# A transformer block with linear attention and eight experts: modulation of the token rows moved behind the dispatch, LayerNorm statistics moved to ScalarE, a running sum moved to GpSimd

## The chip, the cores and the metric

The kernel runs on one core of one Trainium2 chip. The metric is device time in microseconds (us). Before the change the median of six runs is 1135.47 us (1133.32 to 1144.9). Engines are named as in the profile: PE is TensorE (matmul and transpose), PEld its weight loads, DVE is VectorE, ACT is ScalarE, Pool is GpSimd, and SP is SyncE, which here only issues DMAs.

## The reference

There are 8192 tokens (4 batches of 2048) of D = 256 features, all in fp32. Six modulation rows per batch come from the condition c. Then:

```python
mod = (silu(c) @ wmod).reshape(4, 6, 1, 256)
sa, ca, ga, sb, cb, gb = mod[:, 0], ..., mod[:, 5]
ga, gb = sign(ga) * max(|ga|, 0.25), sign(gb) * max(|gb|, 0.25)
h = layernorm(x) * (1 + ca) + sa
q, k, v = phi(h @ wq.T), phi(h @ wk.T), h @ wv.T      # phi = elu + 1, 16 heads of 16
# along each sequence: S += k v^T, z += k, out = (S q) / max(z . q, 1e-6)
x = x + ga * (out @ w_out.T)
h = layernorm(x) * (1 + cb) + sb
gates = softmax(h @ w_router.T)                        # 8 experts, the best 2 of each token,
# 1280 places per expert, given out in token order; the kept gates are made to sum to 1: combine
hidden = silu(h @ w_gate.T)                            # 512 features, shared by the experts
x = x + gb * sum_e combine[:, e] * (hidden @ w_down[e].T)
```

## The kernel before, in words

**Setup.** It loads weights, computes the modulation, and keeps it in three forms: `modc` (columns, for data that has features on partitions), `gab` (rows of ga and gb) and `scb` (rows of sb and 1 + cb).

**Token stage.** The tokens are taken in 16 groups `g` of 512, each of four tiles `j` of 128; four groups make a batch. A loop over steps `s` = (g, j) runs under an order written out by hand for PE, ACT, DVE and Pool: an engine executes its instructions in just the order in which the loop writes them. Step (g, j) does the attention of tile j: `scores` (psc, masked by DVE at L419), `attend` of the step before (po, copied to oT by ACT at L472), `keep_state` (a matmul `pst`, added to the running sum `s_acc` by DVE at L442, then masked to `s_msk` by Pool at L444), and `project_out` (pw at L485, the add into x, and the statistics of the second LayerNorm). Between these stand pieces of other groups, by j:

| step | next group g+1 | g+2 and g+3 | group before, g-1 | g-2 |
|---|---|---|---|---|
| j=0 | q, first running keys | g+2: normalise a (L287) on ACT | spread of the second norm | |
| j=1 | `kk` copies (L354), values | g+3: load of x on SP | normalise m on ACT | `positions` (L574), `dispatch` |
| j=2 | denominators `den` (L382), scaled q (`pr`) | g+2: `hTa` (L300); g+3: statistics on DVE | `hTm`; row inputs of two tiles on Pool | sends of two tiles |
| j=3 | | g+2: k | logits, `ranks` on DVE; row inputs of two tiles | sends of two tiles |

Here a is the first LayerNorm, m the second. Its statistics are bn_stats and bn_aggr on DVE, then `ve` (DVE), the power `rstd` (Pool) and `nmr` (DVE, L278); normalise is one ACT instruction per tile with scale and bias, and the transposes of `to_features` follow on PE, whose copy to SBUF (`hTa`, `hTm`) applies the modulation as columns. Most matmul results of this stage share one PSUM ring, `bank`, of two buffers, so a result that is read late holds up the matmul after the next.

**Rows.** For the experts, `row_inputs` (L491) writes each token's row into `hrow` on Pool: normalised x times 1 + cb plus sb (two operations a tile, L502 and L503), gb, the combine weights and the token number; W = 2D + 12 = 524 floats. `send` (L626) scatters the rows, 128 per indirect DMA on Pool's queue, into `slots` in DRAM, 1280 for each expert. Blank rows are put there first: `free_slots` (L618) issues 80 blocks of 128 rows on SP, eight at each of the steps 2 to 11, each behind the mask of that step. The sends wait for all of them.

**Experts' stage.** Its order is the scheduler's. Each expert has three blocks of 4, 4 and 2 tiles: `rows` are loaded on SP (L646; a ring `e3` of five buffers), DVE casts the token numbers `tok` (L657), Pool gathers the tokens' present output `xc` (L660), PE transposes the rows (`pte`, L676, copied by ACT at L677), then `ph` (L682), tanh on ACT (L690), `hid` on DVE (L691), `pe` (L696), on DVE `y` (L703, times combine weight and gb) and the add of `xc` (L707), and a scatter to the output on Pool (L708).

## Time and profile before

The profiled execution took 1141.07 us, with a span of 1139.3 us and a mean granted clock of 0.919. It counts 17805 instructions. Busy times by stage, from the windows of the trace, in us (share of that stage for PE):

| stretch (us) | PE | DVE | ACT | Pool | clock | DMA share |
|---|---|---|---|---|---|---|
| 0 to 100, setup and start | 72.4 (72%) | 46.2 | 28.3 | 21.7 | 0.91 | 0.16 |
| 100 to 400, tokens | 252.6 (84%) | 198.6 | 123.7 | 148.2 | 0.93 | 0.37 |
| 400 to 700, tokens | 248.0 (83%) | 204.2 | 120.9 | 165.0 | 0.92 | 0.16 |
| 700 to 770, last tokens | 50.3 (72%) | 44.9 | 16.7 | 42.3 | 0.84 | 0.12 |
| 770 to 814, drain | 5.8 (13%) | 11.2 | 3.8 | 22.8 | 0.50 | 0.17 |
| 814 to 1139, experts | 305.2 (94%) | 131.4 | 73.9 | 159.1 | 0.98 | 0.42 |
| whole span | 934.3 (82%) | 636.5 (56%) | 367.3 (32%) | 558.8 (49%) | 0.919 | |

How to read it: an engine is limited by its own work only where its busy time fills the stretch. The clock is that of PE, as a share of full speed. The DMA issues of the page: 80 blank blocks of 262 KB (3.7 us to landing), 16 loads of rows of 1048 KB (7.3 us), 16 loads of x of 512 KB (3.9 us), 128 sends. In all 110.69 MB go through the queues.

### The profile page before, as it was taken

To read this page: it belongs to the slowest core of one execution; us is meant where nothing else is said; L and a number is where in the kernel's file an instruction comes from. 1 tells how busy PE (TensorE), PEld (TensorE's weight loads), DVE (VectorE), ACT (ScalarE), POOL (GpSimd) and SP (SyncE) were. 2 spreads that over 40 slices of the span, in tenths; PEclk is the share of its full clock that TensorE was granted. 3 is DMA by queue.
4 is the path that set the end of the run, shared out by engine and by line. 5 is a ranking of instruction groups with operands and counts; after the bars stand their busy time and mean duration, and the time that the engine had idled before them with its cause. 6 is when DMAs were issued, how large, how long until landed. Compare 5 with 4: busy or idle time off the path is not lost. (4 is left out here: it accounts for less than half of the span.)

```text
span 1139.3 us, 17805 instructions
## 1 busy us (share of the span) xinstructions
PE 934.3 (82%) x6832; PEld 662.2 (58%) x6832; DVE 636.5 (56%) x1448; ACT 367.3 (32%) x738; POOL 558.8 (49%) x690
## 2 busy tenths in 40 slices
PE   5878988788887887887987879762499999999996
PEld 5546666556656555565665566541275666666664
DVE  3446565775676676756767757662243444434443
ACT  0344533344334343444344343111122222221221
POOL 4012343484473663644745636665534555535553
PEclk9889998999898998989989889785699999999998
DMA  5004775221122121211111000011524443544321
GB/s 185 1 1 143 268 247 213 76 95 62 56 92 76 57 95 47 86 50 66 69 45 58 31 32 31 31 33 50 200 85 156 159 158 113 163 164 140 126 76 51
DMA packets 62902, 110.69 MB, mean 97 GB/s; under 512 B 9934, under 2 KB 30670, under 8 KB 62816
## 3 DMA queue, kind: packets, MB, share of 16 engines
q1 hardware_dynamic: 39040, 59.71, 15.7%
q0 software_dynamic: 17920, 42.48, 10.7%
q10 hardware_dynamic: 5856, 7.35, 2.0%
q8 instruction: 54, 0.88, 0.3%
q14 instruction: 32, 0.26, 0.1%
HBM read 47.69 MB, written 74.68 MB: 107 GB/s over the span
## 5 line engine op out<-in xcount | busy, mean ns | idle before, releaser
L696 PE MATMUL pe<-wd,hid 128*128 128x256 f32 x640 | 158.7, 385 | 10.2 <-DVE hid L691 8.3
L626 POOL DMA_INDIRECT slots<-hrow,idx x128 | 131.6, 1028 | 54.3 <-issue 42.5
L419 DVE TENSOR_TENSOR at<-psc,tri 128x1024 f32<-128x1024 f32 x128 | 150.2, 1214 | 13.1 <-PE psc L413 13.0
L682 PE MATMUL ph<-hTe,wg_sb 128*128 128x512 f32 (+1 forms) x384 | 153.3, 527 | 0.0
L485 PE MATMUL pw<-wob,oT 128*128 128x256 f32 x256 | 83.5, 456 | 80.9 <-ACT kk L354 41.9
L444 POOL TENSOR_TENSOR s_msk<-s_acc,bd 128x256 f32<-128x256 f32 x60 | 49.5, 826 | 202.0 <-DVE s_acc L442 197.5
L696 PEld LDWEIGHTS pe<-wd,hid 128*128 128x128 f32 x640 | 116.1, 189 | 54.8 <-DVE y L703 16.1
L708 POOL DMA_INDIRECT out_dram<-y,tok x80 | 78.5, 981 | 95.4 <-DVE y L707 54.2
L485 PEld LDWEIGHTS pw<-wob,oT 128*128 128x128 f32 x256 | 51.3, 215 | 109.2 <-ACT kk L354 35.1
L660 POOL DMA_INDIRECT xc<-out_dram,tok x80 | 80.6, 1007 | 69.7 <-issue 45.4
L690 ACT ACTIVATE th<-ph 128x512 f32<-128x512 f32 (+1 forms) x96 | 50.4, 526 | 189.6 <-PE ph L682 138.7
L682 PEld LDWEIGHTS ph<-hTe,wg_sb 128*128 128x128 f32 x384 | 70.9, 191 | 44.0 <-issue 30.8
L691 DVE SCALAR_TENSOR_TENSOR hid<-th,ph 128x512 f32<-128x512 f32 (+1 forms) x96 | 56.9, 595 | 57.3 <-ACT th L690 49.7
L703 DVE SCALAR_TENSOR_TENSOR y<-pe,rows 128x256 f32<-128x256 f32 x80 | 38.6, 483 | 85.8 <-PE pe L696 61.5
L413 PE MATMUL psc<-qeo,k 32*128 32x256 f32 x1024 | 74.3, 404 | 9.5 <-DVE at L419 9.5
L329 PE MATMUL pv<-wqkv_sb,hTa 128*128 128x256 f32 x256 | 73.6, 451 | 0.9 <-DVE x L486 0.9
L369 POOL TENSOR_TENSOR zq<-zc,q 128x512 f32<-128x512 f32 x32 | 41.4, 1295 | 65.5 <-DVE zc L364 57.2
L464 PE MATMUL po<-at,vpad 128*32 128x128 f32 x2048 | 71.3, 279 | 0.2
L314 PE MATMUL pk<-hTa,wqkv_sb 128*128 128x512 f32 x128 | 65.6, 639 | 5.0 <-ACT rek L320 4.5
L329 PEld LDWEIGHTS pv<-wqkv_sb,hTa 128*128 128x128 f32 x256 | 59.9, 235 | 13.7 <-DVE x L486 1.7
L464 PEld LDWEIGHTS po<-at,vpad 128*32 128x32 f32 x2048 | 53.3, 111 | 22.4 <-issue 21.9
L314 PE MATMUL pq<-hTa,wqkv_sb 128*128 128x512 f32 x128 | 61.4, 605 | 3.7 <-ACT req L320 3.6
(148 smaller groups left out, 1540.4 us busy)
## 6 DMA issues: line engine op xcount, KB each, us to landing
slots<-free SPq DMA_DIRECT2D x80, 262.0 KB, 3.7
rows<-slots SPq DMA_DIRECT2D x16, 1048.0 KB, 7.3
x<-in_x_dram SPq DMA_DIRECT2D x16, 512.0 KB, 3.9
out_dram<-x SPq DMA_DIRECT2D x16, 512.0 KB, 4.5
rows<-slots SPq DMA_DIRECT2D x8, 524.0 KB
wd<-in_wdT_dram ACTq DMA_DIRECT2D x8, 512.0 KB, 4.0
slots<-hrow,idx POOLq DMA_INDIRECT x128
wmod_sb<-in_wmod_dram ACTq DMA_DIRECT2D x1, 1536.0 KB
```

Source lines behind the costliest of these rows:

```text
L314: nc.tensor.matmul(pq, wqkv_sb[:, k, o + h * P : o + (h + 1) * P], hT[:, k, :], start=(k == 0), stop=(k == NH - 1))
L329: nc.tensor.matmul(pv[:, i * D : (i + 1) * D], hT[:, k, (j + i) * P : (j + i + 1) * P], wqkv_sb[:, k, 2 * D : 3 * D], start=(k == 0), stop ...
L413: nc.tensor.matmul(psc[:, a, h], kT[r : r + 32, h, cols], qeo[r : r + 32, h, :, cols], start=True, stop=True,)
L419: masked = nc.vector.tensor_tensor(at, psc[:, 2 * m : 2 * m + 2].rearrange("p i h q t -> p (i h q) t"), tri.unsqueeze(1).to_broadcast([P, ...
L464: nc.tensor.matmul(po[32 * a : 32 * a + 32, h * P : (h + 1) * P], vp[:, j, h * 4 + a, q : q + 2, :], att[a // 2][:, a % 2, h, q, :], start ...
L485: nc.tensor.matmul(pw[:, :D], oT[:, h, :], wob[:, h, :], start=(h == 0), stop=(h == NH - 1))
L626: row = nc.gpsimd.indirect_dma_start(out=slots[:, :], out_offset=bass.IndirectOffsetOnAxis(ap=idx[:, c, j : j + 1], axis=0), in_=hr[:, j, ...
L660: got = nc.gpsimd.indirect_dma_start(out=xc[:, i + j, :], out_offset=None, in_=out[:, :], in_offset=bass.IndirectOffsetOnAxis(ap=tok[:, j ...
L682: nc.tensor.matmul(ph[:, :m], wg_sb[:, k, f * P : (f + 1) * P], hT[:, k, :m], start=(k == 0), stop=(k == NH - 1),)
L691: nc.vector.scalar_tensor_tensor(hid[:, f, :m], th[:, :m], 1.0, ph[:, :m], ALU.add, ALU.mult)
L696: nc.tensor.matmul(pe[:, j, :], hid[:, f, j * P : (j + 1) * P], wds[e][:, f, :], start=(f == 0), stop=(f == NF - 1),)
L708: put = nc.gpsimd.indirect_dma_start(out=out[:, :], out_offset=bass.IndirectOffsetOnAxis(ap=tok[:, j : j + 1], axis=0), in_=y[:, j, :], in ...
```

## The change

1. **Rows.** A row now carries normalised x without modulation, and beside it the batch's rows 1 + cb, sb and gb: W = 4D + 12 = 1036 floats, 4144 bytes for 2096. `gab` and `scb` become one tile `modr`. `row_inputs` is gone; ACT's normalise m writes straight into the row, Pool copies the three modulation rows into it only for the first two groups of a batch (there are two `hrow` buffers). The experts' stage multiplies and adds on DVE ahead of the transposes, two instructions per block, into a new tile `hm`. The ring of row buffers goes from five to four.
2. **Statistics.** Those of the first LayerNorm leave DVE: ACT adds up x (`sums`, an Identity with an accumulated output, for g+3 at j=3), Pool makes the negative mean, ACT adds up the squared differences (`squares`, for g+2 at j=0, where normalise a stood), and Pool makes `ve`, the power and `nmr`. Normalise a moves to j=1, behind the values. The small operations of the second LayerNorm move from DVE to Pool.
3. **State.** ACT copies `pst` to SBUF (`s_add`), and Pool adds it to `s_acc`.
4. **Blank blocks.** `free_slots` moves forward: two batches of eight behind group 0's first k, two behind group 1's, then one at each odd step from 1 to 11.
5. **Room.** relu writes into its destination (no `re` tile), `zq` shares the tile of `qs`, and `ahead` and `tie` have one buffer.

```diff
-O_GB, O_CW, O_TOK, W = D, 2 * D, 2 * D + NE, 2 * D + NE + 4
+O_CB, O_SB, O_GB, O_CW, O_TOK, W = D, 2 * D, 3 * D, 4 * D, 4 * D + NE, 4 * D + NE + 4
...
+    def sums(g):
+        xn = G_["xna", g] = w1.tile([P, NT, D], F32, tag="xna", name=f"xna_{g}")
+        sm = small.tile([P, NT], F32, tag="suma", name=f"suma_{g}")
+        for j in range(NT):
+            nc.scalar.activation(xn[:, j, :], xs[g][:, j, :], AF.Identity, accum_out=sm[:, j : j + 1])
+        nm = small.tile([P, NT], F32, tag="nma", name=f"nma_{g}")
+        nc.gpsimd.tensor_scalar(nm, sm, -1.0 / D, None, ALU.mult)
+    def squares(g):
+        for j in range(NT):
+            nc.scalar.activation(
+                xn[:, j, :], xs[g][:, j, :], AF.Square, bias=nm[:, j : j + 1], accum_out=sq[:, j : j + 1]
+            )
+        nc.gpsimd.tensor_scalar(ve, sq, 1.0 / D, LN_EPS, ALU.mult, ALU.add)
+        nc.gpsimd.tensor_tensor(rstd, ve, mhalf, ALU.pow)
+        nc.gpsimd.tensor_tensor(nmr, nm, rstd, ALU.mult)
...
     def keep_state(g, j):
-            nc.vector.tensor_tensor(flat, flat, pst[:, : NH * P], ALU.add)
+            add = w2.tile([P, NH * P], F32, tag="s_add", name=f"s_add_{g}_{j}")
+            nc.scalar.copy(add, pst[:, : NH * P])
+            nc.gpsimd.tensor_tensor(flat, flat, add, ALU.add)
...
-    def row_inputs(g, j):
-        b, hr = g // GPB, hrows[g % 2]
-        if j == 0:
-            if g % GPB < 2:
-                nc.gpsimd.tensor_copy(
-                    hr[:, :, O_GB : O_GB + D], gab[:, b, 1, :].unsqueeze(1).to_broadcast([P, NT, D])
-                )
-            nc.gpsimd.tensor_scalar(hr[:, :, O_TOK], tok0, float(g * G), None, ALU.add)
-        h2 = hr[:, j, :D]
-        nc.gpsimd.tensor_tensor(h2, G_["xm", g][:, j, :], scb[:, b, 1, :], ALU.mult)
-        nc.gpsimd.tensor_tensor(h2, h2, scb[:, b, 0, :], ALU.add)
+    def second_norm(g):
+        b, hr = g // GPB, hrows[g % 2]
+        if g % GPB < 2:
+            for j in range(NT):
+                nc.gpsimd.tensor_copy(hr[:, j, D : 4 * D], modr[:, b, :3].rearrange("p a d -> p (a d)"))
+        nc.gpsimd.tensor_scalar(hr[:, :, O_TOK], tok0, float(g * G), None, ALU.add)
+        normalise(g, "m", xs.pop(g), hr[:, :, :D])
...
+            hm = e2.tile([P, 4, D], F32, tag="hm", name=f"hm_{e}_{i}")
+            nc.vector.tensor_tensor(hm[:, :n], r[:, :n, :D], r[:, :n, O_CB : O_CB + D], ALU.mult)
+            nc.vector.tensor_tensor(hm[:, :n], hm[:, :n], r[:, :n, O_SB : O_SB + D], ALU.add)
-                    nc.tensor.transpose(pt[:, j * P : (j + 1) * P], r[:, j, h * P : (h + 1) * P], ident)
+                    nc.tensor.transpose(pt[:, j * P : (j + 1) * P], hm[:, j, h * P : (h + 1) * P], ident)
...
-                if 2 <= s < TPE + 2:
-                    free_slots(s - 2, masked)
+                if s % 2 == 1 and 4 + s // 2 < TPE:
+                    free_slots(4 + s // 2, masked)
...
-    e3 = ctx.enter_context(tc.tile_pool(name="e3", bufs=5))
+    e3 = ctx.enter_context(tc.tile_pool(name="e3", bufs=4))
```

## The prediction, as it was put on record before the result

> **What bounds the kernel now.** The busy table by slices comes first. It shows a token stage (to about 770 us) with PE 78 to 89% busy at a granted clock of 0.90 to 0.97, a drain to 814 us, and the experts' stage, PE 95 to 97% busy at 1.00. The profiled run took 1141.07 us (span 1139.3), 5.6 over the median of 1135.47; I sum against 1141.07 and subtract 5.6 at the end.

> Second, PE's waits in a steady stretch of the token stage, 250 to 700 us (us in total, times, longest):

> ```profile
> PE pw L485 <- ACT kk L354: 30.9, 10, 3.3
> PE pw L485 <- DVE den L382: 22.3, 10, 2.2
> PE pta L300 <- ACT hTa L301: 8.7, 10, 0.9
> PE psc L413 <- DVE at L419: 8.5, 7, 1.7
> ```

> That is ten groups of four steps, 45.0 us each (stores of out at 430.67 and 700.55, six groups apart); PE waits 7.9 of it. Third, the timeline around the two large waits:

> ```profile
> 433.46 2.08 ACT L287 ACTIVATE xna<-x,nmra,rstda 128x256 f32<-128x256 f32 x4 [4.43 <-DVE nmra L278]
> 435.44 0.35 ACT L472 COPY oT<-po 128x256 f32<-128x256 f32 x1
> 435.70 1.06 ACT L354 COPY kk<-pk 128x512 f32<-128x512 f32 x2
> 436.42 1.84 PE L485 MATMUL pw<-wob,oT 128*128 128x256 f32 x4 [3.22 <-ACT kk L354]
> ```

> ```profile
> 399.66 0.17 ACT L574 COPY pos<-pp 128x32 f32<-128x32 f32 x1
> 399.86 0.18 DVE L589 TENSOR_SCALAR slot<-pos 128x32 f32<-128x32 f32 x1 [5.84 <-ACT pos L574]
> 402.76 2.35 DVE L419 TENSOR_TENSOR at<-psc,tri 128x1024 f32<-128x1024 f32 x2
> 405.02 0.28 DVE L382 TENSOR_SCALAR den<-pd 128x128 f32<-128x128 f32 x1
> 405.35 1.55 PE L485 MATMUL pw<-wob,oT 128*128 128x256 f32 x4 [2.23 <-DVE den L382]
> ```

> In step 1 ACT idles 4.43 us for a tiny DVE result (nmra), normalises, and only then makes oT and kk, whose PSUM bank PE needs. In step 2 PE needs den's bank, and den stands on DVE behind 3.0 us of routing, itself released by ACT's pos, and the mask (at). Stalls also cost clock (columns: length, then PE, PEld, DVE, ACT, POOL busy, granted clock, DMA share, GB/s):

> ```profile
> 434.00:436.00 2.00, 0.00 (x0) 0.00 (x0) 2.00 (x3) 2.00 (x6) 0.72 (x1) 1.00 0.02 9
> 436.00:438.00 2.00, 1.58 (x4) 1.30 (x5) 0.09 (x1) 0.76 (x2) 0.72 (x1) 0.66 0.00 0
> 438.00:440.00 2.00, 2.00 (x6) 1.57 (x5) 1.67 (x3) 0.00 (x0) 0.00 (x0) 0.50 0.00 0
> ```

> In the experts' stage PE itself is the limit, and one loading wait on DVE already reaches PE:

> ```profile
> 945.34 0.17 DVE L657 CAST tok<-rows 128x4 int32<-128x4 f32 x1 [4.42 <-DMA rows<-slots]
> 946.15 0.70 PE L696 MATMUL pe<-wd,hid 128*128 128x256 f32 x2 [1.47 <-DVE hid L691]
> ```

> **Start: +9.** Before, the first xna starts at 40.82, when the setup's last gab (0.68 us from 39.94) and the copies behind it free the space. DVE loses the 2.2 us in which it waited for rstda at 25.6, so this point comes about 2 us sooner. Then a chain takes the place of statistics already done: four sums on ACT (2.07, the xna row x4), nm on Pool (0.24, row L500), four squares (2.07), ve, power and product on Pool (0.24 + 1.04 + 0.20), some 0.15 for each of four handovers: 6.5. So +4.4. For group 1 the path from qeo's end (65.74) to xna (67.15) was 1.4 us and becomes 6.5: +5. The sums of group 2 (2.07) lie in an ACT gap of 2.29 us before exq at 79.87: nothing.

> **Token stage, steps 0 and 1: about 5 us a group sooner.** Squares stand where the normalise stood, and wait only for nm, done a step earlier: ACT's 4.43 us are used, and kk is ready 0.4 us after pk instead of 3.1. The clock stays up: pw and pv took 1.84 and 4.61 us there against 1.03 and 3.88 (L485 at 415.83, L329 at 704.19 and 706.28), another 1.5. Routing on DVE (ranks) ran 4.0 us at 758.5 without Pool's row work beside it, 5.7 at 421.1 with it; that work is gone, the sums put 1 us of ACT before the exponent: `at` of step 0 ends 1 us sooner, which is most of the 0.85 us wait for it.

> **Step 2: 3 us of it given back.** ACT now runs vpad, normalise a (2.08, moved), normalise m (2.08), pos, oT, the new state copy (0.37), hTa. I went through one group by hand with the rows' durations, from the first scores of step 0. Scores of step 2 start at 18.9 us instead of 23.8 (443.48 less 419.64); pos ends at 22.9 instead of 25.3; den at 28.6 instead of 30.7 to 31; in the compiled order of the changed kernel the first ptm, not pw, waits for den. PE waits here for pos (0.9), hTa (1.0 and 0.9), den (1.6) and hTm (0.9). The next group starts at 43.1 us against 45.0: a gain of 1.9. Groups 0 and 1 have no routing behind pos, and get 3 each.

> **Unknown: the accumulating ACT operation.** No row shows one. Below: 0 more than a plain one (0.52 in a row of four), or 0.1 less, since sums read no scale or bias vector. Above: a further small ACT instruction each, 0.17 (row L574): 0.7 in squares, which delays kk, and 0.7 in sums, which delays ranks; then a group gains 0.5. I take half. Twelve full groups at 1.4 and two at 3: **-23**.

> **The state's sum on Pool: nothing.** Copy 0.37 (row L472) and add 0.78 (rows L502, L503) come before s_msk, which its reader needs a step (11 us) later; Pool sat idle 197.5 us before s_msk. Pool per group: -6.2 (eight row operations), +3.1, +1.3 for small ones, and in half of the groups four copies of 0.8 against one of 1.06. If the add came late, PE would wait in from_state, up to 1 us a step.

> **Free slots: +3 once.** Rows grow from 2096 to 4144 bytes, the 80 blank blocks from 21 to 42 MB. They now start behind the first k (about 55 us, not 98.8) on SP, past the x loads of groups 4 and 5, which have two steps of slack. At 350 GB/s (160 to 170 us, share 1.00) a batch of 4.2 MB takes 12 us of every 22. The sends of step 11 stand in Pool's queue behind that step's batch: Pool waits about 11 us (8.9 in all before), and behind it stand the next s_add, nm and zq; all but 3 us is slack. The sends carry 21 MB more over 600 us, beside a DMA share of 0.17: nothing.

> **Drain: -7.** Eight row operations of 0.72 (781.84 to 792.23) stand between the last sends and are gone: 5.8, and about 1 of the earlier dispatch.

> **First rows: +8.** Before:

> ```profile
> 809.34 67.92 SPq L646 DMA_DIRECT2D rows<-slots  x9
> 814.52 1.94 PE L676 MATMUL pte<-ident,rows 128*128 128x128 f32 x8 [19.91 <-DMA rows<-slots]
> ```

> The block has 2.1 MB instead of 1.05: 3 us at 350 GB/s. Modulation is two DVE operations of 128x1024, each about 1.2 us by the slope of the rows with 256 and 512 elements (0.42, 0.69): 2.4. The second block's pair stands ahead of the first hid: 2.5.

> **Experts: +21.** DVE gets 2 x (1.2 + 1.2 + 0.7) = 6.2 us per expert on 17 of 39.5; much of this falls into its waits for PE. The loads do not. With four buffers, in the compiled order, an expert's first block is requested when the block of two before it, one expert back, gives its last y, and its tok stands on DVE only some 6.5 us of work later.

> ```profile
> DMA to landing us min/median/max: 5.1/7.3/8.5
> ```

> These are loads of 1.05 MB (and half-size ones). Twice the bytes cost 3 us more at 350 GB/s, 7 more if all scales: 8 to 15; I take 10.5, since the queue drains at the former when full. Then the last hid of a block comes about 11 us after the request instead of 8.6; the small block's tok adds 1 to 2. PE waits 3 to 4 us per boundary instead of 1.2, times seven, plus clock: 3 us each, +21. Bounds: +5 (fully hidden), +50 (loads at 15).

> [...]

> *And on clock.* [...] Here it fell to 0.50 (406 to 408 us) after a wait of 2.23 in a sparse stretch. [...]

> **Sum.** +9 - 23 + 3 - 7 + 8 + 21 = +11 on 1141; on the median, **1147**.

> **Rivals.** *Token stage wins (faster).* Two of three large waits start at DVE. If step 2 keeps most of the 5 us (accumulation is free, warm clock through pr, which took 3.19 us cold at 454.70 and 2.37 at 408.63), groups gain 3.5: -50; with loads hidden (+5) the sum is 9 - 50 + 3 - 7 + 8 + 5 = -32: 1104. For it: PE's work per group is 37 us. Against: ACT's longer chain in step 2.
> *ACT becomes the token stage's bound (clearly slower).* With 0.17 more per accumulation or more, and late sends that hold normalise m (it now writes into the rows to be sent), groups gain nothing (+23), and loads land late (+15): about 1185. It decides from some 3 us of squares on.
> *Nothing to measure:* gains and costs cancel, 1135.

> **Numbers.** Forecast 1147 (1141 to 1165): 0.42. Token stage wins: 0.28. ACT bound: 0.16. Cancelling: 0.14. Slower by over 0.5% (5.7 us, about what a measurement tells from no change) 0.58, within 0.14, faster 0.28. The range 1103 to 1185 reaches into both outer cases.

> **What would show it.** Right: the wait of pw for kk gone, ptm waiting for den; first xna normalise near 45 us; groups of 43 to 44 us; last sends closer together; tok waits in the experts' stage of 4 us and more at each boundary, with PE waits behind. Wrong: groups under 42 us, no longer PE waits at boundaries, or squares over 2.8 us per group.

## The result, and the profile after

The changed kernel takes **1145.38 us** (median of 20 runs, 1139.88 to 1149.38); beside it the kernel before took 1136.46 (46 runs). The ratio is 1.0069, with a 95% interval of 1.0052 to 1.0085: slower by 0.7%. The profiled execution has a span of 1146.1 us at a mean granted clock of 0.902. Between the same events in the two traces (us):

| stretch | before | after | measured | predicted |
|---|---|---|---|---|
| start to the normalise a of group 1 | 67.2 | 73.9 | +6.7 | +9 |
| start to the last store of x | 765.4 | 757.2 | -8.2 | +9 - 23 + 3 = -11 |
| to the first request of rows | 43.9 | 36.9 | -7.0 | -7 |
| to the first pte | 5.2 | 10.7 | +5.5 | +8, of which 2.5 behind it |
| to the end of the span | 324.8 | 341.4 | +16.6 | +21 |
| sum of the last four | 1139.3 | 1146.1 | +6.8 | +11 |

PE's waits in the same 450 us of the token stage (us in total, times, longest):

```profile
PE ptm L318 <- DVE den L399: 17.6, 10, 2.1
PE pta L318 <- ACT hTa L319: 8.7, 10, 0.9
PE ptm L318 <- ACT hTm L319: 8.7, 10, 0.9
PE pw L504 <- ACT hTa L319: 8.7, 10, 0.9
PE pta L318 <- ACT pos L589: 6.8, 10, 0.7
```

The 30.9 us in which pw waited for kk are gone (3.6 are left), ptm and not pw now waits for den, and pos, hTa and hTm have become late. Nearly all of it stands in step 2, as predicted, and so does the low clock: over nine groups the mean clock of step 2 is 0.75 in the changed kernel and that of the other steps 0.99 to 1.00, where before it was 0.89 in step 1 and 0.84 in step 2.

In the experts' stage (850 to 1100 us of both traces), first the kernel before, then the changed one:

```profile
DVE tok L657 <- DMA rows<-slots: 33.7, 18, 4.4
PE pe L696 <- DVE hid L691: 8.3, 10, 1.5
```

```profile
DVE tok L672 <- DMA rows<-slots: 21.3, 12, 4.5
DVE y L721 <- DMA out_dram<-y,tok: 9.0, 2, 4.5
PE pe L714 <- DVE y L721: 10.0, 11, 3.5
PE pe L714 <- DVE hid L709: 4.1, 3, 2.8
```

DVE's waits for rows have not grown. What is new is that DVE waits for a scatter before it can write y, and PE for y. PE's longest wait there:

```profile
1010.72 3.78 PE L714 MATMUL pe<-wd,hid 128*128 128x256 f32 x8 [3.55 <-DVE y L721]
```

After it the eight matmuls take 3.78 us, where they take 1.99 at full clock (at 921.06): the wait of 3.55 us costs 5.3.

### The profile page after: what moved, and what is told of

Read it like the earlier page. It is cut to its first block, busy times and chain, and to the rows that moved or that the text cites. A ratio compares the mean times of both kernels' runs of the same rounds, so it can differ in the third digit from the quotient of the medians.

```text
span 1146.1 us, 18139 instructions
## 1 busy us (share of the span) xinstructions
PE 942.8 (82%) x6832; PEld 667.4 (58%) x6832; DVE 621.0 (54%) x1244; ACT 441.6 (39%) x1054; POOL 558.7 (49%) x738
## 5 line engine op out<-in xcount | busy, mean ns | idle before, releaser
L714 PE MATMUL pe<-wd,hid 128*128 128x256 f32 x640 | 162.4, 393 | 19.0 <-DVE y L721 11.3
L714 PEld LDWEIGHTS pe<-wd,hid 128*128 128x128 f32 x640 | 118.4, 193 | 67.5 <-DVE y L721 30.2
L726 POOL DMA_INDIRECT out_dram<-y,tok x80 | 84.0, 1050 | 105.6 <-DVE y L725 48.7
L708 ACT ACTIVATE th<-ph 128x512 f32<-128x512 f32 (+1 forms) x96 | 50.5, 526 | 198.8 <-PE ph L700 173.7
L675 POOL DMA_INDIRECT xc<-out_dram,tok x80 | 84.4, 1055 | 72.1 <-issue 43.1
L461 POOL TENSOR_TENSOR s_acc<-s_acc,s_add 128x256 f32<-128x256 f32 x56 | 40.5, 723 | 124.0 <-ACT s_add L460 117.8
L504 PE MATMUL pw<-wob,oT 128*128 128x256 f32 x256 | 77.6, 430 | 27.6 <-ACT hTa L319 11.4
L700 PEld LDWEIGHTS ph<-hTe,wg_sb 128*128 128x128 f32 x384 | 71.6, 193 | 43.1 <-issue 31.9
L504 PEld LDWEIGHTS pw<-wob,oT 128*128 128x128 f32 x256 | 49.4, 205 | 53.0 <-issue 16.6
L338 DVE SCALAR_TENSOR_TENSOR k<-exk,k 128x512 f32<-128x512 f32 x32 | 22.1, 692 | 88.0 <-ACT k L337 81.3
L483 PEld LDWEIGHTS po<-at,vpad 128*32 128x32 f32 x2048 | 53.2, 109 | 25.3 <-issue 24.9
L318 PE MATMUL ptm<-ident,hrow 128*128 128x128 f32 x128 | 33.4, 407 | 41.2 <-DVE den L399 24.7
L346 PE MATMUL pv<-wqkv_sb,hTa 128*128 128x256 f32 x256 | 58.7, 383 | 0.0
```

The costliest lines, as they stand in the source:

```text
L346: nc.tensor.matmul(pv[:, i * D : (i + 1) * D], hT[:, k, (j + i) * P : (j + i + 1) * P], wqkv_sb[:, k, 2 * D : 3 * D], start=(k == 0), stop ...
L483: nc.tensor.matmul(po[32 * a : 32 * a + 32, h * P : (h + 1) * P], vp[:, j, h * 4 + a, q : q + 2, :], att[a // 2][:, a % 2, h, q, :], start ...
L504: nc.tensor.matmul(pw[:, :D], oT[:, h, :], wob[:, h, :], start=(h == 0), stop=(h == NH - 1))
L675: got = nc.gpsimd.indirect_dma_start(out=xc[:, i + j, :], out_offset=None, in_=out[:, :], in_offset=bass.IndirectOffsetOnAxis(ap=tok[:, j ...
L700: nc.tensor.matmul(ph[:, :m], wg_sb[:, k, f * P : (f + 1) * P], hT[:, k, :m], start=(k == 0), stop=(k == NH - 1),)
L714: nc.tensor.matmul(pe[:, j, :], hid[:, f, j * P : (j + 1) * P], wds[e][:, f, :], start=(f == 0), stop=(f == NF - 1),)
```

## The experiments

Each timed run stands beside the kernel before on its chip (medians 1134.5 to 1138.2). In the table, "group" is the mean of the last eleven intervals between two rden (a group of four steps); the other columns are the stretches of the table above, of the profiled execution.

| kernel | median us | ratio to before (95%) | group | last store | load to pte | experts |
|---|---|---|---|---|---|---|
| before | 1136.5 | | 44.5 | 765.4 | 5.2 | 324.8 |
| changed | 1145.4 | 1.0069 (1.0052 to 1.0085) | 43.6 | 757.2 | 10.7 | 341.4 |
| narrow_rows | 1123.2 | 0.9875 (0.9833 to 0.9917) | 43.5 | 748.9 | 8.3 | 326.3 |
| no_row_modulation | 1141.8 | 1.0030 (1.0003 to 1.0058) | 43.6 | 756.5 | 9.1 | 338.6 |
| tokens_only | 1134.3 | 0.9978 (0.9959 to 0.9997) | 44.3 | 761.9 | 5.2 | 322.3 |
| early_nmr | 1087.9 | 0.9559 (0.9516 to 0.9601) | 41.2 | 714.2 | 5.2 | 324.3 |
| y_four_buffers | 1131.6 | 0.9946 (0.9925 to 0.9967) | 43.2 | 745.9 | 11.8 | 336.5 |
| positions_first | 1092.8 | 0.9607 (0.9585 to 0.9629) | 40.9 | 709.9 | 10.5 | 337.7 |
| dve_statistics | 1095.6 | 0.9653 (0.9603 to 0.9703) | 40.9 | 702.9 | 10.5 | 339.2 |
| early_nmr_positions | 1043.5 | 0.9176 (0.9155 to 0.9197) | 37.7 | 668.6 | 5.3 | 321.7 |
| state_on_dve | 1106.7 | 0.9740 (0.9700 to 0.9780) | 41.4 | 720.4 | 10.7 | 337.5 |
| blank_blocks_early | 1153.5 | 1.0163 (1.0129 to 1.0196) | 43.0 | 764.7 | 10.7 | 338.6 |
| best_from_before | 1039.7 | 0.9163 (0.9134 to 0.9192) | 37.6 | 666.9 | 5.2 | 319.8 |
| best_with_parts_3_to_5 | 1039.8 | 0.9158 (0.9129 to 0.9188) | 39.0 | 669.2 | 5.4 | 321.5 |

**1. Bytes or DVE work.** On the changed kernel:

```diff
+O_CB, O_SB, O_GB, O_CW, O_TOK, W = D, D, D, 2 * D, 2 * D + NE, 2 * D + NE + 4   # one row, gb, in second_norm
```

> The changed kernel with rows of 524 floats again: the row holds normalised x, the gb row, weights and token, and the experts' stage uses gb where it would use 1 + cb and sb, so the batch's modulation of the experts' input is replaced by another one; its two DVE instructions per block and the ring of four row buffers stay. What differs is bytes: 85 MB less through the queues. From the two profiles, the experts' stage (first pte to the end) went from 324.8 to 341.4 us and the load of the first rows to the first pte from 5.2 to 10.7. Theory 1, bytes (the doubled loads land late, or hold up the gathers and scatters beside them): the experts' stage returns to 325 to 329 and the first pte comes 3 us sooner, about 1127. Theory 2, DVE (the added 6.2 us per expert): only the 3 us of the first load are gained, about 1142.

Measured: 1123.2, and an experts' stage of 326.3 us. (The queues carry 110.7 MB for 173.6, so 63 MB less and not 85.) The bytes cost 22 us by the medians; in the profiled executions 15 in the experts' stage, 2.4 ahead of the first pte and 8 in the token stage. The loads land in 5.6 us (median) for 9.0, and DVE's longest wait for rows is 2.7 us for 4.5:

```profile
DVE tok L672 <- DMA rows<-slots: 16.7, 13, 2.7
```

The mirror image left out the two DVE instructions:

```diff
-            nc.vector.tensor_tensor(hm[:, :n], r[:, :n, :D], r[:, :n, O_CB : O_CB + D], ALU.mult)
-            nc.vector.tensor_tensor(hm[:, :n], hm[:, :n], r[:, :n, O_SB : O_SB + D], ALU.add)
```

> The changed kernel with the wide rows and four buffers, without the two DVE instructions per block: the experts take normalised x without the modulation by 1 + cb and sb, which is left out. The mirror image of the kernel with narrow rows. Theory 1, bytes: only the 2.4 us of the first pair are gained and little else, 1141 to 1144. Theory 2, DVE: the experts' stage returns to 325 to 329, about 1128. If both kernels give most of the 16.6 us, the two add up beyond a threshold: a late load costs only what DVE's longer queue does not absorb.

Measured: 1141.8, experts 338.6. DVE's work costs 3.6 us by the medians, the bytes nearly everything. In the experts' stage that work is not told apart from nothing: four other kernels below have it, and two y buffers, and take 337.5 to 339.2 us there. Theory 1 stands as to the cause. By which way the bytes reach PE it does not show.

**2. A ring behind the wide loads.** `tag="y", ... bufs=4` on the changed kernel.

> The changed kernel with four y buffers in the experts' stage for two. In its profile PE's waits there are no longer for hid at the boundary (4.1 us in all for 8.3 before) but for y (11.3 us, longest 3.5): DVE's y waits 4.5 us for a scatter of the block two before, and the matmul after it waits and then runs at half the clock (8 matmuls in 3.78 us for 1.99). Theory: the wide loads hold up the gathers and scatters on Pool's queue, and the ring of two y buffers turns this into a wait of PE; with four, 8 to 14 us come back: 1131 to 1137. Rival: Pool's queue of gathers and scatters itself (some 43 us per expert) is the limit, and y only shows it: 1143 to 1146.

Measured: 1131.6, the number that the theory gave, and not for its reason: that it fits is luck. The experts' stage is 336.5 us; the four kernels below with wide rows and two y buffers have 337.5 to 339.2, so the ring is worth 1 to 3 us, although DVE's waits for a scatter are gone. Eleven of the gain lie ahead of the last store, where PE, DVE, Pool and SP run the same instructions in the same order, and ACT too, except that three loads of expert weights are requested later. The theory of the ring falls; what the eleven are, the section on the hardware says.

**3. The token stage without the wide rows.** Part 1 undone: `row_inputs` again, rows of 524 floats, no `hm`, five buffers.

> Part 1 of the change undone, the rest kept: rows of 524 floats modulated on Pool in the token stage (eight operations a group), five row buffers, no DVE modulation in the experts' stage. Theory: the token stage's gain (8.2 us to the last store of x) comes from ACT's statistics and the order of its work, and stays; drain, first rows and experts return to what they were before: 1136.5 - 8 = about 1128. Rival: Pool's eight operations a group were what slowed the routing on DVE (5.7 us with them, 4.0 without); with them back den is later in step 2 by 1 to 1.7 us a group, and 13 to 20 us are lost: 1136 to 1148.

Measured: 1134.3. Groups are at 44.3 us for 43.5 with narrow rows and no row work on Pool: parts 2 to 5 alone gain nearly nothing, and what gained was the row work off Pool (0.8 us a group, and 6 to 7 in the drain). The rival was nearer; the time lies 2 us below the lower end of its price.

**4. One late operation.** On the kernel before, `nmr` by Pool, behind the power:

```diff
+            nm = small.tile([P, NT], F32, tag="nma", name=f"nma_{g}")
+            nc.gpsimd.tensor_scalar(nm, mv[:, :, 0], -1.0, None, ALU.mult)
+            nc.gpsimd.tensor_tensor(nmr, nm, rstd, ALU.mult)
...
                     spread_of(far, "a")
+                    shift_of(far, "a")
```

> The kernel before with one edit: nmr of the first LayerNorm is made by Pool directly behind the power, a step and a half before it is needed (two operations of 0.2 us for one on DVE); the statistics stay on DVE. It takes away ACT's wait of 4.43 us for nmra in step 1 without any work for ACT. Theory: the token stage's gain needs only this, and without the normalise moved behind the values, pos is not late: den is at 26 to 27 us of the group instead of 28.6, a group gains 2 to 3 us: 1136.5 - 14 x 2.5 = about 1102 (1095 to 1110). Rival, den is given by DVE's own queue and most is given back: a gain like the changed kernel's, 0.6 us a group: about 1128.

Measured: **1087.9**, 49 us less, a little more than the theory. ACT normalises at once (at 442.52 with no wait ahead of it), pw's wait for kk falls from 30.9 us to 2.6, and den's stays as it was:

```profile
PE pw L490 <- DVE den L387: 22.3, 10, 2.2
```

So the wait that the change removed by moving statistics to ACT hung on one operation of 0.2 us in the wrong place of DVE's queue; moving the statistics was not needed. (The edit moves that operation to Pool and ahead at once; an early one on DVE was not tried.) In the changed kernel the same is seen from the other side:

**5. What the moved normalise costs.** On the changed kernel, positions ahead of the normalises:

```diff
+                if old is not None:
+                    positions(old)
+                    dispatch(old)
                 if nrm is not None:
                     normalise(nrm, "a", xs[nrm], G_["xna", nrm])
                 if prv is not None:
                     second_norm(prv)
-                if old is not None:
-                    positions(old)
-                    dispatch(old)
```

> The changed kernel with positions and dispatch put ahead of the two normalises in step 1: ACT's copy pos, for which DVE's routing waits 6.1 us per group (60.6 in ten groups), comes up to 4.2 us sooner. Theory: den in step 2 stands behind routing and mask, so den comes 2 to 4 us sooner and the wait of ptm for den (17.6 us in ten groups), and with it the half clock in ptm and pr behind it, goes: 1.5 to 3 us a group, 1145 - 13 x 2.2 = about 1117. Rival: the normalises end later by 0.2 us only, but the transposes of step 2 wait for hTa's bank instead, and den's place is taken by hTa and hTm: less than 0.5 us a group, 1139 to 1145.

Measured: 1092.8, 53 us less where 28 were expected (39 against y_four_buffers, which like this kernel lacks the gaps of the last section), and not in the expected way. PE's wait for den has not gone. It is longer and stands ahead of pta (250 to 650 us), and the waits of 0.7 to 0.9 us for pos, hTa and hTm are gone:

```profile
PE pta L318 <- DVE den L399: 45.1, 10, 5.9
```

In all PE waits 5.7 us a group for 6.3. The larger part of the gain is clock: step 2 is at 0.83 for 0.75, and PE's busy time falls from 37.3 to 35.2 us a group. Here one long wait cost less clock than several short ones close together.

And with the statistics back on DVE, their small operations on Pool directly behind (`squares(nrm)` and `sums(far)` out, normalise a at step 0):

> The changed kernel with part 2 partly undone: the first LayerNorm's statistics are made by DVE again (at step 2, as before), its small operations stay on Pool directly behind them, and normalise a stands at step 0, where the squares stood; the rest as changed. The kernel before with only an early nmr took 1088, so a late nmr, not the statistics, held the token stage. Theory: the ACT statistics cost about what they save, since ACT's step 1 gets a moved normalise of 2.1 us ahead of pos; without them groups take 40 to 41 us for 43.4, 1145 - 14 x 2.8 = about 1106. Rival: Pool's added work (state sum, small operations) or DVE's is the limit, and groups stay at 43: 1140 or more.

Measured: 1095.6. Both ways groups take 40.9 us: ACT's longer queue ahead of pos is what the change paid for its gain, about 2.6 us a group, with what a late pos brings with it (section 6). On the kernel before with early nmr, the same move of positions:

> The kernel before with nmr made early by Pool, and positions and dispatch ahead of normalise m in step 1. The longest wait left in the token stage with early nmr is pw for den in step 2 (22.3 us in ten groups, 2.2 each, and half clock after it); pos comes 2.1 us sooner. Theory: den's wait goes, and 1 to 2.5 us a group: 1088 - 13 x 1.8 = about 1064. Rival: den waits behind the masks, which wait for PE's scores, not for the routing: 1084 to 1088.

Measured: **1043.5**, 20 us less than the theory. PE's largest wait is now den's 16.3 us in 400; groups take 37.7 us, with 8.95 of 10 us of PE busy and the clock at 1.00 throughout.

**6. The state's sum.** Part 3 undone in the changed kernel:

```diff
-            nc.scalar.copy(add, pst[:, : NH * P])
-            nc.gpsimd.tensor_tensor(flat, flat, add, ALU.add)
+            nc.vector.tensor_tensor(flat, flat, pst[:, : NH * P], ALU.add)
```

> The changed kernel with part 3 undone: DVE adds pst to the state, as before. Theory of the prediction: the state's sum on Pool costs and saves nothing, since s_msk has a step of slack: 1143 to 1148. Rival: ACT's copy and Pool's add lengthen what stands behind them (Pool waits 12.9 us for the blank blocks at step 11, and the adds stand behind), so undoing it saves 3 to 8 us: 1137 to 1142; or DVE's 0.37 us a step back in front of mask and den cost up to 1 us a group: up to 1158.

Measured: 1106.7, 39 us less than the changed kernel by the medians, 37 by the ratios (25 or 23 less than y_four_buffers, whose token stage has no gaps in its last steps either). Neither theory had this size. The timeline of step 2 in the changed kernel shows the cause, Pool's rows among DVE's routing:

```profile
484.49 0.72 POOL L461 TENSOR_TENSOR s_acc<-s_acc,s_add 128x256 f32<-128x256 f32 x1 [0.61 <-ACT s_add L460]
484.61 0.65 DVE L612 TENSOR_TENSOR gates<-gates,keep 128x32 f32<-128x32 f32 x1
485.29 0.73 POOL L463 TENSOR_TENSOR s_msk<-s_acc,bd 128x256 f32<-128x256 f32 x1
485.29 0.19 DVE L614 TENSOR_REDUCE s<-gates 128x4 f32<-128x32 f32 x1
485.51 0.53 DVE L615 TENSOR_SCALAR s<-s 128x4 f32<-128x4 f32 x1
```

DVE's `gates` ends when Pool's add ends, its `s` when Pool's mask ends. From 250 to 650 us, mean ns of one (last but one figure), changed kernel and then with the state on DVE:

```profile
L612 DVE TENSOR_TENSOR gates<-gates,keep 128x32 f32<-128x32 f32 x9 | 5.4, 599 | 0.3
L615 DVE TENSOR_SCALAR s<-s 128x4 f32<-128x4 f32 x9 | 4.7, 521 | 0.3
```

```profile
L610 DVE TENSOR_TENSOR gates<-gates,keep 128x32 f32<-128x32 f32 x10 | 1.9, 192 | 0.3
L613 DVE TENSOR_SCALAR s<-s 128x4 f32<-128x4 f32 x10 | 1.7, 170 | 0.3
```

That is 0.76 us a group in the chain pos, routing, mask, den, behind which PE stands. PE's wait for den is 8.3 us in ten groups with the state on DVE for 17.6, and the clock, low for less long, gives the rest: in the changed kernel it is 0.77 at 486, 0.50 from 488 to 496 and 0.68 at 496; with the state on DVE 0.54 at 471, 0.50 to 477, and 0.75 at 477, some 3 us shorter. A group costs 2.2 us less (1.8 against y_four_buffers). ACT's copy, which the edit takes away too, is not what gained: PE's waits for hTa, hTm and pos, which stand behind it, are the same in both (8.7, 8.7, 8.7 and 6.8 us in ten groups).

The cost hangs on when pos comes. In dve_statistics Pool adds the state in the same way, but the routing runs at another time, and there `gates` takes 192 ns and `s` 170. In positions_first the two take 460 and 333 ns on average. So these gains do not add up, and what the sum on Pool would cost in those orders was not tried.

**7. The blank blocks.** On the changed kernel, batches of blocks at steps 0 to 5:

```diff
-                if s % 2 == 1 and 4 + s // 2 < TPE:
-                    free_slots(4 + s // 2, masked)
+                if 4 + s < TPE:
+                    free_slots(4 + s, masked)
```

> The changed kernel with the last six batches of blank blocks at the steps 0 to 5 for 1, 3, 5, 7, 9 and 11. In the changed kernel's profile Pool waits 12.9 us at 202 us for the last batch, and PE behind it 6.2 (for kk): the group there takes 50.5 us between two rden; with narrow rows in the same order it takes 44.9, with a Pool wait of 7.1. Theory: the wait of the sends costs 5 to 6 us once, and goes when all blocks are in DRAM by then (12 us for each 4.2 MB): 1139 to 1141. Rival: the transfers only move to the loads of x of groups 4 to 6 on the same queue, and the same microseconds are lost there: 1143 to 1148.

Measured: 1153.5; the rival, and worse. The load of x for a later group stands on SP's queue behind the blank blocks, 42 MB in all (it is issued at 170.16 us, behind the last of them), and ACT's sums wait for it:

```profile
ACT xna L260 <- DMA x<-in_x_dram: 28.5, 1, 28.5
```

**8. The best that came of it.** Three edits on the kernel before (early nmr, positions first, three y buffers):

> The kernel before with nmr made early by Pool, positions and dispatch ahead of normalise m, and three y buffers in the experts' stage. With two y buffers it took 1043.5. Theory: with narrow rows PE waits for y 0.6 us in all, so a third buffer gives nothing: 1041 to 1045. Rival: where the ring limits Pool's scatters, up to 5 us: 1038 to 1041.

Measured: 1039.7, 8.4% below the kernel before. By the medians the third buffer gives 3.8 us, by the ratios to the kernel before on each chip 1.5, within their intervals (the experts' stage is 319.8 us for 321.7): the two guesses are not told apart. With parts 3 to 5 of the change on top:

> The same three edits on the changed kernel without part 1 and without ACT's statistics: the statistics on DVE, all small operations on Pool directly behind them, the state's sum by ACT and Pool, blank blocks early, rows narrow and modulated on Pool in the token stage. Theory: DVE, busy 78% of the token stage in the kernel with early nmr and positions first, loses 0.37 us a step and the small operations, so den's last wait (1.6 us a group) shrinks: 5 to 15 us less, 1028 to 1038. Rival: PE is at 89% at full clock there, and Pool's longer queue (66% busy already) delays zq or the sends: 1043 to 1055.

Measured: 1039.8, no difference; groups are slower by 1.4 us and the first ones, with the blank blocks early, faster (38.5 us for 48.1 in the one where the sends start).

## Why the prediction came out as it did

The forecast was 1147 and the time 1145.4. Every stretch has the predicted sign, and the sums differ by 4 us. In the token stage and the drain the predicted waits are those of the trace. That the total is so near is in part luck: a term put at nothing cost 23 to 39 us, PE's gaps of the last section were not foreseen, and the experts' term came about in another way. By its steps:

- **Start, +9: measured +6.7.** The first normalise came 2.0 us later, not 4.4; the second as predicted (4.8 for 5). The 0.15 us for a handover were the author's estimate; the four of the first group take 0.04 to 0.09 (38.61 to 42.77 us).
- **Steps 0 and 1, 5 us sooner: held.** From the first scores of step 0 to those of step 2 it is 18.0 us for 22.6 (means of nine groups). The wait for kk fell to 3.6 us in eleven, and pv took 379 ns for 465 on average.
- **The accumulating operation: the lower bound.** An accumulation is two instructions, the activation and a read of the accumulator, and the next activation starts before the read ends:

```profile
515.40 0.51 ACT L270 ACTIVATE xna<-x,nma 128x256 f32<-128x256 f32 x1
515.80 0.20 ACT L270 ACTIVATION_READ_ACCUMULATOR xna<-x,nma 128x1 f32 x1
515.89 0.51 ACT L270 ACTIVATE xna<-x,nma 128x256 f32<-128x256 f32 x1
```

```profile
483.65:487.06 3.41, 1.46 (x9) 0.99 (x10) 2.73 (x12) 2.24 (x6) 1.68 (x3) 1.00 0.52 147
487.06:490.47 3.41, 2.15 (x6) 1.24 (x7) 3.31 (x7) 0.00 (x0) 2.08 (x2) 0.50 0.28 108
```

  PE is busy 1.46 of 3.41 us, and the next three such stretches, to 497.30, have half the clock. Behind 100 us this trace has 21 such falls. In the 3.41 us ahead of each PE was busy for 49% or less, and in eleven of them no wait was longer than 0.9 us; no stretch at full clock that another one followed was less busy than that. (In the kernel before, behind 100 us too, the falls came after 43% or less, and a stretch at full clock in which PE was busy for 44% was followed by another one.)

## What to carry to other kernels

Before work is moved to another engine because its result is late, look whether it is late in doing or in the queue: here one 0.2 us operation, moved ahead, gave 49 us, and the order of one ACT copy another 44 (some of it the gaps of the next section, of which only the first of these two kernels has any). Work given to Pool is charged to the DVE instructions that run at the same time (here 599 ns for 192 and 521 for 170), by their own chain, not by the slack of Pool's result. Short waits of PE that fall close together are charged with the clock behind them (here 0.50 after waits of 0.7 to 0.9 us). And data that travels through DRAM to save two vector operations pays for its bytes on every trip: 22 us here, for 7 saved in the drain and 0.8 a group.

## What the runs showed of the hardware that was not expected

In the profiles of before, the changed kernel, narrow_rows, no_row_modulation, tokens_only and early_nmr, PE has short idle times that nothing released, near the last steps up to 2.8 us (2.82 ahead of the pw at 763.57 in the kernel before). In the changed kernel the sixteen matmuls `pl` of the last group run from 744.4 to 750 us with gaps of 0.3 to 1.0 us, where they take 1 us in y_four_buffers:

```profile
745.28 0.45 PE L526 MATMUL pl<-hTm,wr 128*32 128x128 f32 x5 [0.58 <-issue]
746.72 0.38 PE L526 MATMUL pl<-hTm,wr 128*32 128x128 f32 x3 [0.99 <-issue]
```

The other eight programs have none. In the changed kernel it is worth some 8 to 11 us (from the last rden to the last store of x 50.5 us, in y_four_buffers 42.9); in the kernel before less, if early_nmr_positions is the measure (48.9 for 44.1). So part of the 0.7% by which the change is slower may be this. It follows the program, not the edit: differences of less than it between two kernels of which only one has it prove nothing, and the gains of positions_first, dve_statistics and state_on_dve against the changed kernel are smaller by about this much (39, 36 and 25 us against y_four_buffers). What causes it was not tried and stays open.
